# A conditioned block on one core: block 0's inner features in another tile, two groups of operations swapped, one weight load on another queue, weight sums at other places

## The chip, the core and the metric

The kernel runs on one core of one Trainium2 chip. Its time is device microseconds of one execution, taken several times; the median counts. One more execution is recorded by the hardware profiler, and everything said of engines and waits comes from that record. The core has five engines that run side by side, each through its own list of instructions in order: TensorE (PE, the matmuls), VectorE (DVE), ScalarE (ACT), GpSimd (POOL) and SyncE (SP, which here only starts transfers). ACT can start transfers too. [...]

## What is computed

Four sequences' worth of tokens, 2 x 2048 rows of 512 features, go through a block whose scales, shifts and gates come from a condition vector:

```python
emb = jnp.dot(jax.nn.silu(t), ada_w) + ada_b
shift_msa, scale_msa, gate_msa, shift_mlp, scale_mlp, gate_mlp = jnp.split(emb, 6, axis=-1)
norm = _ln(x) * (1.0 + scale_msa[:, None]) + shift_msa[:, None]
h = jax.nn.gelu(jnp.dot(norm, ssm_w1) + ssm_b1, approximate=False)
ssm_out = jnp.dot(h, ssm_w2) + ssm_b2
x = x + gate_msa[:, None] * ssm_out
norm2 = _ln(x) * (1.0 + scale_mlp[:, None]) + shift_mlp[:, None]
hf = jax.nn.gelu(jnp.dot(norm2, ff_w1) + ff_b1, approximate=True)
ff_out = jnp.dot(hf, ff_w2) + ff_b2
x = x + gate_mlp[:, None] * ff_out
```

`ssm_w1` and `ssm_w2` are 512 x 512, `ff_w1` is 512 x 1024, `ff_w2` 1024 x 512, all in float32.

## The kernel before, in words

The 4096 rows are cut into 8 blocks of 512 tokens; blocks 0 to 3 belong to the first sequence, 4 to 7 to the second. A block goes through four products, which the code names by letters: hA (first weight, exact gelu), oA (second weight, added to x), hC (ff's first weight, approximate gelu) and oC (ff's second weight, added to x). Each is done with seven products of half size in place of eight (P1 to P7), for which sums of the operands' quarters are formed beforehand: `sums_of_first` (lines 309 to 312) and `sums_of_second` (319 to 322), four additions each. The seven go in the order P1, P2, P6, P5, P7, P3, P4; in block 0's hA it is P1, P2, P5, P6, P3, P7, P4, and `FIRST` (P1, P2, P5, P6, P7, P3, P4) in block 0's oA and block 1's hA. P1, P6, P7 and P4 accumulate in the PSUM bank "y", P5 and P3 in "v", P2 in "x"; after each one DVE adds the bank's content to its destination (lines 554 to 566 in a hidden product, 598 in a residual one), and the next product of the same bank may start only when that is done.

The order is written out by hand: every engine carries out its instructions in the order in which the code emits them. A dictionary `hooks` holds, for each of P1 to P7, the operations to be emitted right after that product's matmuls; `hook` spreads a list over given places, one each, the last place taking the rest. So the places in the hooks are the places in the lists of DVE, ACT, POOL and SP.

From block 1 on, hC uses a scheme with fewer products over registers (`HK_A`, `HK_B`, `HK_P`): `HK_A` is a program of 37 additions of 128 x 256 elements that turns ff_w1 and its earlier sums, in place, into the combinations that the scheme needs. It runs once, on DVE (`sums_of_registers`, lines 631 and 633), and overwrites fw1_sb and fw1_s; because fw1_sb has already been turned into sums for block 0's hC, ff_w1 is first loaded a second time into the same tile (`load_w` at line 927, 2 MB, on SP). The list `fa_sums` holds the 37; `take(n)` emits the next n: 22 in block 0's oC (line 954), 8 in block 2's hA (line 1007), the rest in block 1's hC. `HK_B` does the like for the tokens, on POOL (also line 633), in the tile `forms`, from block 1 on.

The tiles that matter here:

- `big_tile` gives one of 8 rotating buffers of 1 MB for x, the slices of ada_w, the normalised tokens nT and the inner features hA, hClo, hChi. A new tile waits for the last reader of the buffer's earlier one. Block 0's hA takes one at line 800, right before ada_5.
- `forms` is a tile of its own, not used before block 1.

Around the change stand, in time's order: block 0's hA (to 32 us) with the gate row (`rows_of_gates(2)`: L283 on PE, L292 on DVE, then the matmul `pgate`, L298); block 0's oA with block 1's statistics (`stats`, L419 and L420 on DVE), scales (`scales`, L428 to L446, ten small operations on POOL), normals (`normal`, L459 on ACT), transposes (L488 on PE) and modulation (L502); POOL's sums of w2's and fw1's quarters; block 1's hA from 49 us; then block 0's hC, block 1's oA, block 0's oC (101 to 127 us), block 2's hA. Block 2's normalised tokens nT_2 are turned by DVE (L470) and moved by 16 transfers of 64 KB on SP (`move`, L479); then ACT modulates them (L502). Block 1's second norm, n2_1, goes the same way in block 0's oC, with its 16 moves shared by SP and ACT.

Transfers carry one of eight semaphores in turn, and one that takes a semaphore again waits for the one before on it.

Of the kernel before, what the change touches and what calls it, by code (L numbers as in the profile page):

```python
# [140 lines left out]
def kernel(  # L141
# [16 lines left out]
    nc = tc.nc  # L158
    P = 128
    B, N, D = x.shape  # L160
    H = fw1.shape[1]
    KD = D // P
# [30 lines left out]
    def big_tile(name):  # L193
        return big.tile([P, KD, D], F32, tag="big", name=name)
# [11 lines left out]
    def load_ada(g):  # L206
        ada[g] = big_tile(f"ada_{g}")
        nc.sync.dma_start(
            out=ada[g], in_=ada_w[:, g * D : (g + 1) * D].rearrange("(k p) n -> p k n", p=P)
        )  # L210

    def load_w(name, w, t=None):
        if t is None:
            t = const.tile([P, w.shape[0] // P, w.shape[1]], F32, tag=name, name=name)
        nc.sync.dma_start(out=t, in_=w.rearrange("(k p) n -> p k n", p=P))
        return t

    def load_row(t, row):
# [14 lines left out]
    load_ada(0)  # L233
    load_ada(1)
    w1_sb = load_w("w1", w1)
    load_ada(2)

    nc.gpsimd.memset(brows[:, :2, :], 0.0)
    for n, g in enumerate((2, 5)):
        nc.scalar.dma_start(  # L240
            out=brows[:B, n, :], in_=ada_b[g * D : (g + 1) * D].unsqueeze(0).to_broadcast([B, D])
        )
    w2_sb = load_w("w2", w2)
    b2_bc = work.tile([P, D], F32, tag="gb", name="gb2_0", bufs=2)
    load_row(b2_bc, b2)
    load_x(1)
    load_ada(3)
    load_ada(4)
    fw1_sb = load_w("fw1", fw1)

    mods = {}

    def modulation(g0, part):


        g = g0 + part
        pa = ps_g.tile([P, D], F32, tag="x", name=f"pada_{g}")
        w = ada[g].rearrange("p k (n m q) -> p k m n q", n=KD, q=G)
        for k in range(KD):
            for m in range(P // G):  # L260
                nc.tensor.matmul(
                    pa[m * G : (m + 1) * G, :P],
                    silu[:, k, :],
                    w[:, k, m],
                    start=(k == 0),
                    stop=(k == KD - 1),
                    tile_position=(0, m * G),
                    skip_group_check=True,
                )
        turned = work.tile([P, KD, G], F32, tag="turned", name=f"turned_{g}")  # L270
        nc.vector.transpose(turned.rearrange("p n q -> p (n q)"), pa[:, :P])
        m = const.tile([P, KD, B], F32, tag=f"mod_{g0}_{part}", name=f"mod_{g0}_{part}")
        bias = colsT[:, R_ADA + g * KD : R_ADA + (g + 1) * KD]
        nc.vector.tensor_tensor(m, turned[:, :, :B], bias.unsqueeze(2).to_broadcast([P, KD, B]), ALU.add)
        mods[g0, part] = m
# [124 lines left out]
    def hook(hooks, places, ops):  # L400

        for n, op in enumerate(ops):
            hooks.setdefault(places[min(n, len(places) - 1)], []).append(op)
# [180 lines left out]
    def residual(name, i, hops, wops, kdim, hooks, last=False, order=ORDER):  # L584

        xt = xs[i]
        F = D // 2
        q = {
            "11": xt[:, 0:2, :F],
            "12": xt[:, 0:2, F:],  # L590
            "21": xt[:, 2:4, :F],
            "22": xt[:, 2:4, F:],
        }
        dest = {"P1": "11", "P2": "11", "P6": "12", "P5": "22", "P7": "22", "P3": "12", "P4": "21"}

        def after(p, ps, js):
            d = q[dest[p]][:, js]
            nc.vector.tensor_tensor(d, ps[BANK[p]][:, js], d, ALU.add)  # L598
            if last and p in ("P7", "P4"):
                s = slice(2 + js.start, 2 + js.stop)  # L600
                f = slice(F, D) if p == "P7" else slice(0, F)
                nc.sync.dma_start(out=out_blk[i][:, s, f], in_=xt[:, s, f])

        parted = ("P1", "P6", "P7", "P4") if last else ()
        group(name, kdim, hops, lambda p, j, k: wops[p][:, k, :], after, hooks, parted, order)
# [16 lines left out]

    forms = const.tile([P, 16, C, HT // C], F32, tag="forms", name="forms")

    def sums_of_registers(program, reg, engs):


        def op(n, d, f, a, b):
            eng = engs[n % len(engs)]
            if f == "n":  # L630
                nc.vector.scalar_tensor_tensor(reg[d], reg[a], -1.0, reg[b], ALU.mult, ALU.subtract)
            else:
                eng.tensor_tensor(reg[d], reg[a], reg[b], ALU.add if f == "+" else ALU.subtract)  # L633

        return [lambda z=(n,) + step: op(*z) for n, step in enumerate(program)]
# [93 lines left out]
    def run(ops):  # L729
        for op in ops:  # L730
            op()
# [4 lines left out]
    n1 = {0: Norm(0, 1), 1: Norm(1, 1)}  # L736
# [60 lines left out]
        n1[0].modulate(k, pts[k], nc.vector if k % 2 else None)  # L797
    n1_sums = n1[0].summed(nc.vector)
    run(n1_sums[:2])
    hA_0 = big_tile("hA_0")  # L800
    load_ada(5)
    fw2_sb = load_w("fw2", fw2)
    gb, hA = {2: b2_bc}, {}
# [9 lines left out]
    def fold2(lo, hi):  # L813
        return [lambda k=k: found["w2"][1][k]() for k in range(lo, hi)]

    hooks = {}
    hook(hooks, ("P1",), n1_sums[2:3])
    hook(hooks, ("P2",), [lambda: rows_of_gates(2)] + n1_sums[3:])
    st = n1[1].stats()
    hook(hooks, ("P5",), [ssm_gate, gb2_0] + biases(0, b2_bc) + fold2(0, 1))  # L820
    hook(hooks, ("P6",), fold2(1, 7))
    hook(hooks, ("P3", "P7"), st)
    hook(hooks, ("P7",), [lambda: modulation(3, 0)])
    hA[0] = First(0, n1[0].ops, hooks, ("P1", "P2", "P5", "P6", "P3", "P7", "P4"), hA_0)
    w2_ops = found["w2"][0]

    hA_sums = hA[0].summed(nc.vector)
    hooks = {}
    hook(hooks, ("P1",), [n1[1].scales] + fold2(7, 8) + hA_sums[:2])
    hook(hooks, ("P2",), hA_sums[2:] + [lambda c=c: n1[1].normal(c, on_pe=True) for c in range(C)])  # L830
    hook(hooks, ("P6",), [lambda: modulation(3, 1)])
    hook(hooks, ("P7", "P3", "P4"), n1[1].turned())
# [1 line left out]
    st = n2[0].stats()  # L834
# [7 lines left out]
    hooks = {}  # L842
# [37 lines left out]
    def take(n):  # L880
        ops = fa_sums[:n]
        del fa_sums[:n]
        return ops

    n1[2] = Norm(2, 1)
    for i in range(NBLK):
        nxt, nx2, last = i + 1 < NBLK, i + 2 < NBLK, i + 1 == NBLK
        hC = Second(i)
        if i == 0:
            hooks = first_hooks  # L890
# [3 lines left out]
            hooks = {}  # L894
# [9 lines left out]
        else:  # L904
            hooks = {}
# [16 lines left out]
        hooks = {}  # L922
        hook(hooks, EARLY, hC.summed(1, nc.gpsimd if nxt else nc.vector))
        if nxt:

            if i == 0:
                hook(hooks, ("P1",), [lambda: load_w("fw1", fw1, fw1_sb)])
                fa_sums.extend(sums_of_registers(HK_A, fa, (nc.vector,)))
            if nx2:
                hook(hooks, ("P7",), n1[i + 2].moved())  # L930
            if fold:
                hook(hooks, EARLY, fold[4:8])
                hook(hooks, ("P7",), fold[8:])
            n2[i + 1] = Norm(i + 1, 2)
            hook(hooks, ("P3", "P4"), n2[i + 1].stats())
            residual(f"oA_{i + 1}", i + 1, hA[i + 1], w2_ops, KD // 2, hooks)
        else:
            for p in EARLY:
                run(hooks.get(p, ()))
        fold = None  # L940

        hooks = {}
# [8 lines left out]
            hook(hooks, turns, [lambda c=c: n2[i + 1].turn(c) for c in range(C)])  # L951
            hook(hooks, turns[-1:], [lambda: n2[i + 1].move((nc.sync, nc.scalar))])
        if i == 0:
            hook(hooks, ("P2",) * 2 + ("P6",) * 3 + ("P5",) * 5 + ("P7",) * 6 + ("P3",) * 6, take(22))
        elif i + 3 < NBLK:
            hook(hooks, ("P5", "P7", "P3", "P4"), n1[i + 3].stats())
            hook(hooks, ("P4",), [n1[i + 3].scales])
# [18 lines left out]
        if nxt:  # L976
            late = {}

            def form(eng):

                fb[i + 1] = n2[i + 1].registers()
                return sums_of_registers(HK_B, fb[i + 1], (eng,))

            if not nx2:
                hook(hooks, ("P7",) * 9 + ("P3",) * 6 + ("P4",), [lambda n=n: late_form(n) for n in range(len(HK_B))])

                def late_form(n):
                    if n == 0:
                        late["ops"] = form(nc.vector)
                    late["ops"][n]()  # L990
# [11 lines left out]
        hooks = {}  # L1002
        if refold5:
            hook(hooks, ("P6",), [multiply_5])
        if i == 0:
            hook(hooks, ("P5", "P7", "P3", "P4"), n1[i + 3].stats())
            hook(hooks, ("P1", "P2", "P2", "P6", "P6", "P5", "P7", "P3"), take(8))
        if refold2:
            w2_ops, w2_fold = weight_of_second(w2_sb, w2_s, gate[2, b], (nc.vector,))
            hook(hooks, ALL, w2_fold)  # L1010
# [47 lines left out]
```

## Time and profile before

| | |
|---|---|
| median of 3 runs | 608.75 us (608.74 to 609.2) |
| the profiled execution | 609.73 us, its span 607.9 us |
| PE busy | 98% of the span |
| DVE, ACT, POOL busy | 61%, 35%, 65% |
| DMA queue q1 (SP) | 45.63 MB, 22.1% of 16 engines |
| DMA queue q10 (ACT) | 3.70 MB, 2.4% |

A line of the timeline reads: start in us from the span's start, duration in us, engine, line of the kernel, operation, output tile <- input tiles, shapes, number of instructions, and in brackets the time that the engine stood idle before it with what ended that idle time. A line of the waits reads: engine, output tile and line, what it waited for, then us in total, how often, longest. Buffer numbers are left out of names, so hA is that of any block and fw is any of the tiles of ff_w1 and ff_w2. A wait on several semaphores is put down to the one that came last by the record.

### The profile page before, as it was taken

Reading aid. Unit: us, or ns where it says so; the run is one execution under the profiler, and the core shown is the slowest. Engines: PE = TensorE matmul, PEld = TensorE weight load, DVE = VectorE, ACT = ScalarE, POOL = GpSimd, SP = SyncE. Lnnn points to the kernel's source line nnn. Section 1 sums busy time; section 2 is a strip of 40 time slices with the busy share of each in tenths; the row PEclk is TensorE's granted clock in tenths of the full one; section 3 lists DMA queues with packets and bytes.
Section 4 is the critical chain, followed back from the end, with each engine's and each line's share of the span. In section 5 each row is a group of like instructions: output and inputs, shape, how many; then the busy total and the mean of one; then the engine's idle time right before and its main releaser. Section 6 shows DMA issues by size and latency. Waiting matters only on the chain.

```text
span 607.9 us, 8128 instructions
## 1 busy us (share of the span) xinstructions
PE 593.7 (98%) x2843; PEld 511.4 (84%) x2843; DVE 371.1 (61%) x638; ACT 214.7 (35%) x355; POOL 394.7 (65%) x446
## 2 busy tenths in 40 slices
PE   7999999989999999999999999999999999999997
PEld 3678888778888888888888888888888888888886
DVE  4887785799754456555755458744575236467642
ACT  2233341134711455322642337213553225212420
POOL 2796589878736598438997398895993695540110
PEclk9999999999999999999999999999999999999999
DMA  8971005410132102430042520321020300012001
GB/s 323 414 269 70 1 2 183 159 73 1 27 112 71 69 2 64 162 104 36 1 98 81 159 98 18 122 65 74 1 52 18 104 36 0 1 44 96 1 1 70
DMA packets 22605, 49.85 MB, mean 82 GB/s; under 512 B 4084, under 2 KB 4640, under 8 KB 21668
## 3 DMA queue, kind: packets, MB, share of 16 engines
q1 hardware_dynamic: 19792, 45.63, 22.1%
q10 hardware_dynamic: 2772, 3.70, 2.4%
q8 instruction: 23, 0.38, 0.3%
q14 instruction: 18, 0.15, 0.1%
HBM read 27.29 MB, written 8.39 MB: 59 GB/s over the span
## 4 chain that ended last, share of the span: by engine, by line
PE 79%; DVE 10%; POOL 5%; DMA 2%; issue 2%; ACTq 1%; ACT 0%; SPq 0%; DVEq 0%; POOLq 0%
PE py_oC L385 14%; PE px_hC L694 9%; PE pv_hC L694 8%; PE py_hA L385 8%; PE py_oA L385 8%; PE py_hC L694 7%; PE pv_oC L385 7%; PE pv_oA L385 4%; PE px_oC L385 3%; PE pv_hA L385 3%; PE px_hA L385 2%; DMA ada<-in_L_cond_ada_w_dram 2%; PE px_oA L385 2%; DVE fw L633 1%; DVE fw_s L633 1%
## 5 line engine op out<-in xcount | busy, mean ns | idle before, releaser
L610 POOL TENSOR_TENSOR x<-x,gb 128x512 f32<-128x512 f32 x64 | 80.0, 1280 | 7.6 <-ACT hA L557 3.8
L502 ACT ACTIVATE nT<-nT,mod,mod 128x512 f32<-128x512 f32 x50 | 36.7, 803 | 122.0 <-DMA nT<-blocks 112.0
L459 ACT ACTIVATE nT<-x,nmr,rstd 128x512 f32<-128x512 f32 x52 | 39.6, 804 | 58.1 <-POOL nmr L446 42.2
L428 POOL TENSOR_SCALAR ve<-mv 128x4 f32<-128x4 f32 x16 | 3.7, 233 | 86.2 <-DVE mv L420 86.0
L385 PE MATMUL py_oC<-fw_s,hSC 128*128 128x256 f32 x256 | 57.9, 379 | 0.0
L385 PEld LDWEIGHTS py_oC<-fw_s,hSC 128*128 128x128 f32 x256 | 48.6, 190 | 6.6
L309 POOL TENSOR_TENSOR hSC<-hClo 128x512 f32<-128x512 f32 x15 | 19.1, 1275 | 47.7 <-ACT hClo L689 38.6
L419 DVE BATCH_NORM_STATS2 st<-x 128x6 f32<-128x512 f32 x64 | 43.4, 678 | 5.7 <-DMA x<-in_x_dram 5.4
L598 DVE TENSOR_TENSOR x<-py_oC,x 128x512 f32<-128x512 f32 (+1 forms) x36 | 22.6, 630 | 37.5 <-PE py_oC L385 37.1
L694 PE MATMUL py_hC<-forms,fw 128*128 128x256 f32 x168 | 40.8, 379 | 0.0
L705 DVE TENSOR_TENSOR hClo<-hClo,py_hC 128x512 f32<-128x512 f32 x42 | 28.7, 682 | 17.5 <-ACT hClo L708 9.1
L470 DVE STREAM_TRANSPOSE blocks<-nT 128x512 f32<-128x512 f32 x52 | 35.2, 695 | 5.1 <-ACT nT L459 4.7
L633 POOL TENSOR_TENSOR forms<-forms 128x256 f32<-128x256 f32 x48 | 35.4, 737 | 2.8
L694 PEld LDWEIGHTS py_hC<-forms,fw 128*128 128x128 f32 x168 | 31.9, 190 | 4.3
L598 DVE TENSOR_TENSOR x<-py_oA,x 128x512 f32<-128x512 f32 x32 | 22.1, 690 | 21.2 <-PE py_oA L385 19.3
L705 DVE TENSOR_TENSOR hChi<-hChi,pv_hC 128x512 f32<-128x512 f32 x35 | 23.4, 684 | 16.9 <-PE pv_hC L694 16.9
L385 PE MATMUL py_hA<-nS,w_s 128*128 128x256 f32 x128 | 30.4, 380 | 1.7 <-POOL forms L633 1.7
L385 PE MATMUL pv_oC<-fw,hSC 128*128 128x256 f32 x128 | 29.0, 380 | 1.4 <-DVE x L598 1.4
L385 PE MATMUL py_oA<-w_s,hSA 128*128 128x256 f32 x128 | 30.3, 380 | 0.0
L385 PEld LDWEIGHTS py_hA<-nS,w_s 128*128 128x128 f32 x128 | 24.2, 190 | 6.6 <-POOL forms L633 2.1
L689 ACT ACTIVATE hClo<-hClo,colsT 128x256 f32<-128x256 f32 x56 | 25.4, 500 | 11.8 <-DVE hClo L705 11.7
L385 PE MATMUL px_oC<-fw,hChi 128*128 128x256 f32 x128 | 28.9, 379 | 0.0
(206 smaller groups left out, 1431.3 us busy)
## 6 DMA issues: line engine op xcount, KB each, us to landing
nT<-blocks SPq DMA_DIRECT2D x152, 64.0 KB, 2.0
fw<-in_L_cond_ff_w_dram SPq DMA_DIRECT2D x4, 2048.0 KB, 9.0
out_dram<-x SPq DMA_DIRECT2D x15, 512.0 KB, 3.1
x<-in_x_dram SPq DMA_DIRECT2D x7, 1024.0 KB, 7.1
ada<-in_L_cond_ada_w_dram SPq DMA_DIRECT2D x6, 1024.0 KB, 10.5
nT<-blocks ACTq DMA_DIRECT2D x56, 64.0 KB, 2.1
w<-in_L_cond_ssm_w_dram SPq DMA_DIRECT2D x3, 1024.0 KB, 7.8
x<-in_x_dram SPq DMA_DIRECT2D x2, 512.0 KB, 5.9
```

Source lines behind the costliest of these rows:

```text
L309: lambda: eng.tensor_tensor(s[1], q["11"], q["21"], ALU.subtract),
L385: nc.tensor.matmul(ps[b][j * apart][:, j, :], lhs(p, j, k), rhs(p, j, k), start=(fresh and j * (not apart) == 0 and k == 0), stop=(p in (" ...
L419: nc.vector.bn_stats(st, xs[self.i][:, c, :])
L459: nc.scalar.activation(t, x_c, AF.Identity, bias=self.nmr[:, c : c + 1], scale=self.rstd[:, c : c + 1])
L470: nc.vector.transpose(self.bl[:, :, :, c, :].rearrange("p m k q -> p k m q"), self.nT[:, c, :].rearrange("p (k m q) -> p k m q", k=KD, m=C),)
L502: nc.scalar.activation(dst, src, AF.Identity, bias=shift, scale=scale)
L598: nc.vector.tensor_tensor(d, ps[BANK[p]][:, js], d, ALU.add)
L610: lambda c=c: nc.gpsimd.tensor_tensor(xs[i][:, c, :], xs[i][:, c, :], gb, ALU.add)
L633: eng.tensor_tensor(reg[d], reg[a], reg[b], ALU.add if f == "+" else ALU.subtract)
L689: nc.scalar.activation(h, h, AF.Gelu_apprx_tanh, bias=fb1T[:, m : m + 1])
L694: nc.tensor.matmul(ps[b][:, j, :], fa[ra][:, j * P : (j + 1) * P], fb[rb].rearrange("p a (c q) -> p c a q", q=Q), start=(fresh and j == 0) ...
L705: nc.vector.tensor_tensor(dest(d), dest(d), ps[b], op)
```

## The change

There are five edits. Block 0's hA no longer takes a big tile but the first half of `forms`. In the hooks of block 0's hA only two of block 1's four statistics stay; the other two go to the head of P1's hooks of oA, ahead of the scales; and the first two sums of hA_0, which stood behind the scales and one weight sum in those hooks, are emitted right after hA. The second load of ff_w1 is started by ACT instead of SP. The first 22 of the `HK_A` sums in block 0's oC go to P1 (6), P5 (7), P7 (7) and P3 (2), where they were at P2 (2), P6 (3), P5 (5), P7 (6) and P3 (6). In block 2's hA seven are taken instead of eight (one at P6 less).

```diff
-    def load_w(name, w, t=None):
+    def load_w(name, w, t=None, eng=nc.sync):
...
-        nc.sync.dma_start(out=t, in_=w.rearrange("(k p) n -> p k n", p=P))
+        eng.dma_start(out=t, in_=w.rearrange("(k p) n -> p k n", p=P))
...
     forms = const.tile([P, 16, C, HT // C], F32, tag="forms", name="forms")
+
+    hA_0 = forms[:, :8].rearrange("p n a r -> p (n a r)").rearrange("p (k t) -> p k t", k=KD)
...
     run(n1_sums[:2])
-    hA_0 = big_tile("hA_0")
     load_ada(5)
...
-    hook(hooks, ("P3", "P7"), st)
+    hook(hooks, ("P3", "P7"), st[:2])
...
     hA_sums = hA[0].summed(nc.vector)
+    run(hA_sums[:2])
     hooks = {}
-    hook(hooks, ("P1",), [n1[1].scales] + fold2(7, 8) + hA_sums[:2])
+    hook(hooks, ("P1",), st[2:] + [n1[1].scales] + fold2(7, 8))
...
-                hook(hooks, ("P1",), [lambda: load_w("fw1", fw1, fw1_sb)])
+                hook(hooks, ("P1",), [lambda: load_w("fw1", fw1, fw1_sb, nc.scalar)])
...
-            hook(hooks, ("P2",) * 2 + ("P6",) * 3 + ("P5",) * 5 + ("P7",) * 6 + ("P3",) * 6, take(22))
+            hook(hooks, ("P1",) * 6 + ("P5",) * 7 + ("P7",) * 7 + ("P3",) * 2, take(22))
...
-            hook(hooks, ("P1", "P2", "P2", "P6", "P6", "P5", "P7", "P3"), take(8))
+            hook(hooks, ("P1", "P2", "P2", "P6", "P5", "P7", "P3"), take(7))
```

On the engines this moves the following. DVE: in block 0 the order becomes two statistics, the turn and sum of mod_3_0 (L271, L274), hA_0's two sums (L309, L310), L598 of P1, two statistics, L598 of P2, L311, L312. ACT: the load stands between the last activation of block 0's hC (L570) and the modulation of nT_2 (L502). SP: its list loses the load, and the eighth of nT_2's 16 moves takes the semaphore that the load carries, so it waits for the load to land. PE and POOL keep their order.

## The prediction

> **What bounds the kernel now.** I read the page first: busy shares, then the waits of PE, longest first, and last the timeline of 12 to 64 us and 95 to 150 us, where every one of those waits lies. PE is busy for 593.7 of 607.9 us, so nothing but its 14 us of idle time can be won, and only the part that this change touches. All times below are us from the span's start.
>
> ```profile
> PE 593.7 (98%) x2843; PEld 511.4 (84%) x2843; DVE 371.1 (61%) x638; ACT 214.7 (35%) x355; POOL 394.7 (65%) x446
> ...
> PE py_hA L385 <- POOL forms L633: 1.7, 1, 1.7
> ...
> PE pv_oC L385 <- DVE x L598: 1.4, 1, 1.4
> ...
> PE pgate L298 <- DVE grows L292: 1.2, 1, 1.2
> PE pv_oA L385 <- POOL rstd L444: 1.0, 1, 1.0
> ```
>
> These four waits (5.3 us) are the change's whole field. The timeline names the true causes:
>
> ```profile
> 20.10 0.69 DVE L554 TENSOR_TENSOR hA<-py_hA,colsT 128x512 f32<-128x512 f32 x1 [1.20 <-PE pada L283]
> 23.19 1.13 PE L298 MATMUL pgate<-grows,pick_bc 128*128 128x512 f32 x2 [1.23 <-DVE grows L292]
> ...
> 36.26 0.69 DVE L310 TENSOR_TENSOR hA<-hA 128x512 f32<-128x512 f32 x1 [0.53 <-DVE hSA L309]
> 37.09 1.97 PE L385 MATMUL pv_oA<-w,hA 128*128 128x256 f32 x8 [1.04 <-POOL rstd L444]
> 37.37 0.25 POOL L446 TENSOR_SCALAR nmr<-nmr 128x4 f32<-128x4 f32 x1
> ...
> 42.14 2.35 POOL L310 TENSOR_TENSOR fw<-fw 128x1024 f32<-128x1024 f32 x1
> 42.22 2.30 DVE L274 TENSOR_TENSOR mod<-turned,colsT 128x8 f32<-128x8 f32 x1
> ...
> 47.02 2.37 POOL L312 TENSOR_TENSOR fw_s<-fw,fw_s 128x1024 f32<-128x1024 f32 x1
> ...
> 50.01 0.69 DVE L319 TENSOR_TENSOR nS<-nT 128x512 f32<-128x512 f32 x1 [1.08 <-ACT nT L502]
> ...
> 108.10 0.69 DVE L598 TENSOR_TENSOR x<-px_oC,x 128x512 f32<-128x512 f32 x1 [2.69 <-PE px_oC L385]
> ...
> 119.81 3.72 PE L385 MATMUL pv_oC<-fw,hSC 128*128 128x256 f32 x16 [1.39 <-DVE x L598]
> ...
> 131.36 0.67 DVE L554 TENSOR_TENSOR hA<-py_hA,colsT 128x512 f32<-128x512 f32 x1
> 132.18 1.97 PE L385 MATMUL py_hA<-nS,w_s 128*128 128x256 f32 x8 [1.74 <-POOL forms L633]
> ```
>
> To be seen: hA_0 lies in ada_2's buffer, so DVE may not write it until PE's L283 has read ada_2 (1.20 idle), and the gate row L292 and pgate come late. pv_oA starts 0.14 after DVE's L310 ends (36.95), so L310 is what it waits for; POOL's rstd is a chance neighbour. At 132.18 it is DVE's L554 that frees PSUM bank y, late because L633 sums stand ahead of it. And L274, a tiny operation, takes 2.30 beside a big POOL one, and ends with it.
>
> **What the Trainium skill says.** "SBUF — State Buffer", section "SBUF: two separate sides": GpSimd and a DVE operation with two SBUF inputs take one port pair as an exclusive lock for the whole instruction; the other blocks. The trace agrees: L274 ends 0.03 after POOL's L310; 512-element operations end 0.55 after the POOL operation (L320 18.90 against 18.35, L312 39.83 against 39.29), the 256-element sums L633 about 0.26 after, one per POOL operation (116.27, 1.49 long). L598 reads PSUM and is never blocked (0.68 throughout). "DMA: Bandwidth & Descriptors", section "Issuing engines are not separate DMA queues": transfers issued by ACT and SP run on the same 16 engines and interleave. No stretch of before has a large load on ACT's queue.
>
> **Part 1, hA_0 into forms.** L554 waits for py_hA alone. DVE: L554 18.93 to 19.6; L321 behind POOL's L311 (ends 20.03) to 20.58; L556, L292 to 21.85. pgate can start at 21.96, when PE is free: the 1.23 goes, and all up to oA_0's P2 is 1.24 earlier. No load is late for that: x_1 landed by 22.0, ada_3 by 24.5. Every later big tile takes the buffer one place earlier in the rotation; the waits that follow are for ada loads long landed, and x_2's load (48.08) goes out about 7 earlier, needed at 69. Worth 0.
>
> **Part 2, statistics and sums swapped** (times with the 1.24 taken off). DVE's statistics of c=1 end at 30.13. L271 to 30.35; L274 behind POOL's L320 to 31.53; L309 to 32.2 (or 33.4 if POOL takes the lock first); L310 to 33.9 to 34.1. pv_oA may start at 34.8: no wait. But then L598, two statistics (0.86 each), L598 and only then L311, ending at 37.4 to 37.6, where P6 wants it at 36.4: a new stall of 1.0 to 1.2 for the 1.04 removed. Worse, mv of block 1 is complete at 36.1 to 36.4, where before it stood at 32.95 and POOL was the later (34.18). POOL's scales (3.07 uncontended, L428 at 106.12 to L446 at 109.19; 0.3 more for collisions) end at 39.3 to 39.85, against 37.62. ACT's four normals (2.93) end about 42.7; the first transposes want the last at 42.4: 0.3. Behind the scales on POOL stand L322 of w2 (1.28) and four sums of fw1 (9.7: four of 2.4 and gaps), so these end at N + 11.0 = 50.3 to 50.85, before 49.39. There lies the price: block 1's L319 is ready at 48.9 and before found POOL idle; now the last fw1 sum has the lock, L319 ends 0.55 after it, 50.85 to 51.4, before 50.70. From L319 to L559 (56.74) DVE ran without a gap, and PE's P7 at 56.80 waited for L559. So P7 moves by +0.15 to +0.7: I take +0.45. All of part 1's gain is gone, and block 0 to 105 runs 0.45 late: n2_0's scales, normals and transposes follow the same chain.
>
> **Part 3, fw1 on ACT's queue** (before's times again; the 0.45 shifts all). ACT is free at 89.94, and has nothing to do until L502 at 101.77. SP's issue of the same load took 0.52; first packets came 1.2 after it, all had landed 8.0 after it. With seven moves of 64 KB between them (0.45 MB at about 0.35 MB/us, half of it counted): landing at 98.6. SP no longer issues it, so x_3's load is issued after the moves alone. But the built order has a new wait: the semaphore of the eighth nT_2 move is fw1's, so SP holds moves 8 to 16 until fw1 has landed: 98.6 instead of 94.43. Behind it on SP stand nine moves and x_3's load; for the moves ACT's L502 waits. L502 moves from 101.77 to 105.9, ends 108.9. Its cover: n2_1's normals could not start before 109.23. Cost 0, with 0.6 in hand; beyond that each us goes into the normals.
>
> **Part 4, sums spread.** Six L633 sums go into the 2.69 idle before 108.10: the first behind POOL's hSC (106.04) to 106.3, five of 0.44 to 108.5. POOL's scales lose 0.35, normals start at 109.55, turns end at 113.65 (115.5 before, no sums between them), moves and forms follow 1.9 earlier (forms 123.6). L598 of P5 at 115.0: the 1.39 at P3 goes. The next seven sums meet POOL's four L610: four end one per L610 (to 120.75), three of 0.42 to 121.95; L598 of P7 ends 122.6, P4 wanted 121.7: new stall 0.9; P4 stands at 122.6, before 123.37. Seven more: four free, three at 0.85 beside forms, to 126.45; L598, two sums, L598, L554 to 129.75. P6 of hA_2 then starts at 129.8 to 131 (before 132.18): the unlucky end is when forms start before the sums are through. P7 and P4 keep it: P4 at 137.3 to 138.5, before 139.59: gain 1.1 to 2.3, I take 2.0. hA_2 has seven sums for eight; the one that moves into hC_1 stands beside POOL's hSA: 0.2 back. Net -1.8.
>
> **Sum.** +0.45 - 1.8 = -1.35 on the profiled execution's 609.73 (span 607.93 and 1.80 around it): 608.4. The median of the runs is 0.98 below that execution: 607.4.
>
> **Rivals.** (a) No change to be measured: the sums get no free lock. The seven after P5 and seven after P7 are both slowed by POOL (0.85 to 1.37 each), part 4 brings 1.1 - 0.2, part 2 costs 0.45 to 0.7: 608.3. For: the lock decides twice within 0.3 us. Against: forms come earlier only if the turns do, and then POOL's L610 is as early. (b) Slower: the fw1 load on ACT's ring shares 16 engines with the moves, and SP's moves wait for it. Place: SP's eighth move. If it lands at 101.5 rather than 98.6, normals and turns start 1.8 late and part 4 keeps 0.4; from there each us is paid in full by turns, sums and L598 of P6, which stand in one line on DVE. Landing at 103.5 (5 us lost): +0.45 + 2.0 - 0.4 = +2.05, 610.8. For: such sharing was never run in before. Against: fw1 is 6.4 us of packets and the seven moves 1.2. (c) POOL done earlier: if the collisions fall kindly and fw1's sums end by 48.9, L319 is not blocked, part 1 stays won (-1.2), and with part 4 it gives 605.8. Against: it needs at least 1.4 us out of a chain of 11.
>
> **Numbers.** 0.2% (1.22 us) is about what a measurement of this kernel can tell from no change. Forecast 0.42 (own range 606.4 to 608.0; 0.39 of it counts as faster, 0.03 as same), (a) 0.32, (b) 0.20, (c) 0.06. Faster 0.45, same 0.35, slower 0.20. The range runs from (c) to short of (b)'s full price: 605.6 to 609.9.
>
> **What would show it.** Right: no wait of pgate or pv_oA; a wait of py_oA on DVE's L311 near 37; POOL's last fw1 sum past 50 and DVE's L319 long (over 2 us) beside it; py_hA at about 57.3; SP's moves in two bursts with a hole of 4 us; no wait of pv_oC, one of py_oC's P4 below 1.2. Wrong: L319 short (then c), L502 for nT_2 later than 106.6 after the shift (then b), or P6 of hA_2 not earlier than 131.5 (then a). A wait in blocks 2 to 7, whose code is unchanged, would upset the whole sum.

## The result and the profile after

| | median | lowest to highest | runs |
|---|---|---|---|
| before | 609.0 us | 607.41 to 609.34 | 8 |
| changed | 607.16 us | 606.9 to 607.58 | 8 |

The ratio is 0.9974, its 95% interval 0.9963 to 0.9984. A second, larger set (20 executions of the changed kernel, 33 of the one before) gave 607.07 against 608.67 and a ratio of 0.9981 [0.9973, 0.999]. The change makes the kernel faster by 0.2 to 0.3%. The profiled execution took 607.58 us, with a span of 605.8.

The page's busy line and then the waits of PE, both of the changed kernel. A wait gives us in total, how often, and the longest. Lines of the code below the new hA_0 have moved down by two (the sums are L633 and L635 now, two lines of one helper, and hC's product is L696).

```profile
PE 593.8 (98%) x2843; PEld 511.2 (84%) x2843; DVE 370.9 (61%) x638; ACT 214.8 (35%) x355; POOL 394.7 (65%) x446
```

```profile
PE py_oA L385 <- DVE hSA L311: 0.8, 1, 0.8
PE px_hC L696 <- DVE hChi L707: 0.7, 2, 0.5
...
PE pv_hA L385 <- DVE nT L320: 0.6, 1, 0.6
PE py_oC L385 <- DVE x L598: 0.6, 1, 0.6
PE py_hA L385 <- DVE hA L559: 0.6, 1, 0.6
PE px_hC L696 <- DVE hClo L707: 0.5, 1, 0.5
```

PE's work is the same 593.8 us. The four waits shown of before (pgate 1.2, pv_oA 1.0, pv_oC 1.4, py_hA 1.7) are gone. Five smaller ones, 3.1 us in all, stand in their place: for L311, L320, L598, L559 and hClo. The two of px_hC for hChi were there before as well, with 0.6. The timeline of the changed kernel shows the places, in the order of the steps:

```profile
20.92 1.12 PE L298 MATMUL pgate<-grows,pick_bc 128*128 128x512 f32 x2
...
35.06 0.23 POOL L428 TENSOR_SCALAR ve<-mv 128x4 f32<-128x4 f32 x1 [2.85 <-DVE mv L420]
...
36.29 1.97 PE L385 MATMUL py_oA<-w_s,hSA 128*128 128x256 f32 x8 [0.78 <-DVE hSA L311]
...
46.99 2.36 POOL L312 TENSOR_TENSOR fw_s<-fw,fw_s 128x1024 f32<-128x1024 f32 x1
47.66 2.24 DVE L319 TENSOR_TENSOR nS<-nT 128x512 f32<-128x512 f32 x1 [1.08 <-ACT nT L502]
...
50.68 1.99 PE L385 MATMUL pv_hA<-nT,w 128*128 128x256 f32 x8 [0.64 <-DVE nT L320]
...
55.99 1.99 PE L385 MATMUL py_hA<-nS,w_s 128*128 128x256 f32 x8 [0.59 <-DVE hA L559]
...
88.30 0.41 ACTq L215 DMA_DIRECT2D fw<-in_L_cond_ff_w_dram  x1
...
97.88 5.57 SPq L479 DMA_DIRECT2D nT<-blocks  x9
...
104.51 0.97 DVE L635 TENSOR_TENSOR fw<-fw 128x256 f32<-128x256 f32 x1
105.10 2.94 ACT L502 ACTIVATE nT<-nT,mod,mod 128x512 f32<-128x512 f32 x4 [15.97 <-DMA nT<-blocks]
...
108.54 2.94 ACT L459 ACTIVATE nT<-x,nmr,rstd 128x512 f32<-128x512 f32 x4 [0.51 <-POOL nmr L446]
...
121.66 3.72 PE L385 MATMUL py_oC<-fw_s,hChi 128*128 128x256 f32 x16 [0.60 <-DVE x L598]
...
128.71 1.97 PE L385 MATMUL py_hA<-nS,w_s 128*128 128x256 f32 x8
```

To be seen: pgate starts without a wait (an idle time would stand in brackets). POOL sat idle 2.85 until block 1's mv was complete, so its last fw1 sum runs to 49.35, and DVE's L319, ready at 47.66, is held for 2.24 in place of 0.69 and ends 0.55 after POOL's. DVE's next operations are late with it: P5 of hA_1 (50.68) waits 0.64 for L320, and P7 (55.99) 0.59 for L559. In the second half, SP has issued seven of nT_2's 16 moves by 93.59 and the other nine from 97.88 on, when ACT's load has landed (97.87). In before the same nine followed the first seven at once:

```profile
94.43 5.65 SPq L479 DMA_DIRECT2D nT<-blocks  x9
```

ACT finishes L502 for nT_2 and waits 0.51 more for POOL before the normals: the late moves were covered, with half a microsecond to spare. P6 of hA_2 (128.71) has no stall.

**A ledger.** PE is busy 98% of the span, so a shift of its products tells where time is won. For each of PE's groups of products (some 340) I took its start in a kernel's timeline minus that in the timeline of before, and noted where the difference steps. The start of the run is left out: the profiled execution of before reached its first transposes 0.92 us later than that of the changed kernel, through its first loads, and some executions start later still (last section). That is no effect of the change.

```
us, change of PE's shift     changed  part 1  parts 1+2  parts 3+4
pgate                         -1.36   -1.40    -1.38       0
P5 of oA_0 (pv_oA)            -1.20   -0.43    -1.20       0
P6 of oA_0, then to 44        +1.13    0       +1.12       0
P5 to P7 of hA_1 (50 to 57)   +1.54    0       +1.54       0
P3 of oC_0                    -1.56    0        0         -1.56
P4 of oC_0, P1 of hA_2        +0.76    0        0         +0.76
P6 of hA_2                    -1.87    0       -0.42      -1.98
P4 of hA_2                    -0.51    0       -0.50      -0.50
hC_1 (150 to 155)             +1.21    0       +0.32      +1.33
block 7, px_hC                +0.32   +0.25    +0.09      -0.28
```

The rows of the changed kernel come to -1.54, with the start to about -2.5; the spans differ by 2.15, since the stretch after PE's last product was 0.35 us longer than in before. The steps of one edit repeat from kernel to kernel within 0.15 us. The last row does not: two profiled executions of the changed kernel agree within 0.1 us from the first transposes up to there and then part by 0.75, at a wait of px_hC for ACT's hClo of which one shows 0.7. No edit touches that place. Medians and ledger of one execution can therefore differ by about 1 us, and I use the ledger for where, and medians of one set of runs for how much.

### The profile page after: what moved, and what is told of

Same layout as the page of the kernel before. It is cut to its first block, busy times and chain, and to the rows that moved or that the text cites. A ratio compares the mean times of both kernels' runs of the same rounds, so it can differ in the third digit from the quotient of the medians.

```text
span 605.8 us, 8128 instructions
## 1 busy us (share of the span) xinstructions
PE 593.8 (98%) x2843; PEld 511.2 (84%) x2843; DVE 370.9 (61%) x638; ACT 214.8 (35%) x355; POOL 394.7 (65%) x446
## 4 chain that ended last, share of the span: by engine, by line
PE 86%; DVE 8%; DMA 2%; issue 1%; ACTq 1%; ACT 1%; POOL 0%; SPq 0%; DVEq 0%
PE py_oC L385 15%; PE px_hC L696 9%; PE py_oA L385 9%; PE py_hA L385 8%; PE pv_hC L696 8%; PE pv_oC L385 7%; PE py_hC L696 7%; PE pv_oA L385 4%; PE pv_hA L385 4%; PE px_oC L385 4%; PE py_hC L385 2%; PE px_oA L385 2%; PE px_hA L385 2%; DMA ada<-in_L_cond_ada_w_dram 2%; PE pv_hC L385 1%
## 5 line engine op out<-in xcount | busy, mean ns | idle before, releaser
L502 ACT ACTIVATE nT<-nT,mod,mod 128x512 f32<-128x512 f32 x50 | 36.7, 802 | 123.1 <-DMA nT<-blocks 114.7
L309 POOL TENSOR_TENSOR hSC<-hClo 128x512 f32<-128x512 f32 x15 | 19.1, 1277 | 48.7 <-ACT hClo L691 38.9
L598 DVE TENSOR_TENSOR x<-py_oC,x 128x512 f32<-128x512 f32 (+1 forms) x36 | 22.6, 630 | 37.6 <-PE py_oC L385 37.2
L696 PE MATMUL py_hC<-forms,fw 128*128 128x256 f32 x168 | 41.1, 380 | 0.0
L635 POOL TENSOR_TENSOR forms<-forms 128x256 f32<-128x256 f32 x48 | 35.8, 747 | 2.8
L696 PEld LDWEIGHTS py_hC<-forms,fw 128*128 128x128 f32 x168 | 31.8, 190 | 4.7 <-DVE hClo L707 0.4
L598 DVE TENSOR_TENSOR x<-py_oA,x 128x512 f32<-128x512 f32 x32 | 22.1, 690 | 21.2 <-PE py_oA L385 19.6
L385 PE MATMUL py_oC<-fw_s,hChi 128*128 128x256 f32 x128 | 29.0, 380 | 0.6 <-DVE x L598 0.6
```

The lines of the kernel that those rows point to most:

```text
L309: lambda: eng.tensor_tensor(s[1], q["11"], q["21"], ALU.subtract),
L385: nc.tensor.matmul(ps[b][j * apart][:, j, :], lhs(p, j, k), rhs(p, j, k), start=(fresh and j * (not apart) == 0 and k == 0), stop=(p in (" ...
L502: nc.scalar.activation(dst, src, AF.Identity, bias=shift, scale=scale)
L696: nc.tensor.matmul(ps[b][:, j, :], fa[ra][:, j * P : (j + 1) * P], fb[rb].rearrange("p a (c q) -> p c a q", q=Q), start=(fresh and j == 0) ...
```

## The experiments

Two theories stood behind the first four. A is the chain of the prediction: late statistics, late scales on POOL, the port lock at L319, a small net for the start; and the gain in the spread sums. B put it elsewhere, as each expectation says. The first four ran beside one set of the kernel before (608.28 us median, 42 executions).

**1. Part 1 alone.**

```diff
+    hA_0 = forms[:, :8].rearrange("p n a r -> p (n a r)").rearrange("p (k t) -> p k t", k=KD)
...
-    hA_0 = big_tile("hA_0")
```

> Part 1 alone (hA_0 in forms). Theory A (the lock chain): pgate no longer waits, and since block 1's statistics, POOL's scales and fw1's sums keep their places, POOL is idle when block 1's L319 starts; the 1.2 to 1.36 us stay won to the end: 1.2 us faster than before, hA_1's P7 some 1.3 earlier. Theory B (the gain of block 0 is absorbed somewhere before 105 us whatever part 2 does): 0 us.

Measured: 607.37 us, ratio 0.9986 [0.9978, 0.9993]. pgate moves by 1.40, pv_oA by another 0.43, and nothing is given back: no further step of the ledger reaches 0.1 us before block 7, so the new rotation of the big tiles cost nothing that PE saw. The timeline of this kernel, where the statistics keep their place:

```profile
31.80 0.23 POOL L428 TENSOR_SCALAR ve<-mv 128x4 f32<-128x4 f32 x1
...
44.77 2.36 POOL L312 TENSOR_TENSOR fw_s<-fw,fw_s 128x1024 f32<-128x1024 f32 x1
47.22 0.69 DVE L319 TENSOR_TENSOR nS<-nT 128x512 f32<-128x512 f32 x1 [1.08 <-ACT nT L502]
```

POOL gets mv at 31.80 and not at 35.06, its last sum is over at 47.13, and L319 at 47.22 takes 0.69. It escapes by 0.09 us.

**2. Parts 1 and 2.** To the edit of experiment 1 comes

```diff
-    hook(hooks, ("P3", "P7"), st)
+    hook(hooks, ("P3", "P7"), st[:2])
...
+    run(hA_sums[:2])
...
-    hook(hooks, ("P1",), [n1[1].scales] + fold2(7, 8) + hA_sums[:2])
+    hook(hooks, ("P1",), st[2:] + [n1[1].scales] + fold2(7, 8))
```

> Parts 1 and 2 (tile and swap), load and sums as before. Theory A: both waits (pgate, pv_oA) are gone and both come back, at P6 of oA_0, P5 and P7 of hA_1, because POOL's fw1 sums end late and hold the port against L319: 0 us (from -0.3 to +0.4) against before, 1.2 slower than part 1 alone. Theory B (the swap is worth its 1.0 us): 2.2 us faster than before.

Measured: 609.05 us, ratio 1.0019 [1.001, 1.0028]. Part 2 thus costs 609.05 - 607.37 = 1.68 us. The ledger has the same swing by 57 us: from -1.83 with part 1 to +0.08; by the end of the run the two are 1.2 us apart. Its timeline shows the lock as in the changed kernel:

```profile
46.98 2.36 POOL L312 TENSOR_TENSOR fw_s<-fw,fw_s 128x1024 f32<-128x1024 f32 x1
47.64 2.24 DVE L319 TENSOR_TENSOR nS<-nT 128x512 f32<-128x512 f32 x1 [1.07 <-ACT nT L502]
```

Compared with before, the two parts together are a loss of 0.77 by the medians, outside theory A's range, where the ledger's rows come to -0.43. That difference stays open.

**3. Parts 3 and 4.**

```diff
-                hook(hooks, ("P1",), [lambda: load_w("fw1", fw1, fw1_sb)])
+                hook(hooks, ("P1",), [lambda: load_w("fw1", fw1, fw1_sb, nc.scalar)])
...
-            hook(hooks, ("P2",) * 2 + ("P6",) * 3 + ("P5",) * 5 + ("P7",) * 6 + ("P3",) * 6, take(22))
+            hook(hooks, ("P1",) * 6 + ("P5",) * 7 + ("P7",) * 7 + ("P3",) * 2, take(22))
...
-            hook(hooks, ("P1", "P2", "P2", "P6", "P6", "P5", "P7", "P3"), take(8))
+            hook(hooks, ("P1", "P2", "P2", "P6", "P5", "P7", "P3"), take(7))
```

> Parts 3 and 4 (fw1's second load on ACT, sums spread, 7 for 8), tile and order of block 0 as before. Theory A: all that the change wins lies here: 3.2 us won up to hA_2's P4, 1.2 given back in block 1's hC, 2.0 us faster than before. Theory B (the profile's gain is mostly in the start of the run and in block 0): under 0.5 us.

Measured: 606.49 us, ratio 0.9972 [0.9961, 0.9983], 1.79 us below before. By the ratios, practically the whole gain of the change is in these two parts.

**4. The changed kernel without part 2.**

```diff
-    hook(hooks, ("P3", "P7"), st[:2])
+    hook(hooks, ("P3", "P7"), st)
...
-    run(hA_sums[:2])
...
-    hook(hooks, ("P1",), st[2:] + [n1[1].scales] + fold2(7, 8))
+    hook(hooks, ("P1",), [n1[1].scales] + fold2(7, 8) + hA_sums[:2])
```

> The changed kernel with part 2 undone (parts 1, 3, 4). Theory A: -1.2 and -2.0 add up: 3.2 us faster than before, 1.3 faster than the changed kernel; L319 of block 1 takes 0.7, not 2.2. Theory B (the swap is worth 1.0): 0.8 to 1.0 slower than the changed kernel.

Measured: 605.63 us, ratio 0.9963 [0.9949, 0.9976]. It is 0.86 below parts 3 and 4 alone, as part 1 was 0.91 below before, and 1.5 below the changed kernel, which ran in another set; L319 again takes 0.69.

**5. Is it the chain on POOL, or only late normals?** In the changed kernel POOL idles 2.85 us while a ready sum of w2 (L322) stands behind the scales. Here it goes ahead of them:

```diff
-    hook(hooks, ("P1",), st[2:] + [n1[1].scales] + fold2(7, 8))
+    hook(hooks, ("P1",), st[2:] + fold2(7, 8) + [n1[1].scales])
```

> The changed kernel, with POOL's sum of w2 (L322, 1.3 us) put ahead of block 1's scales, into the 2.85 us for which POOL waits for mv. Theory A (part 2 loses by a chain on POOL: late scales, then L322, then four sums of fw1 that hold the port lock when L319 is ready): the last fw1 sum ends about 1.3 us earlier (48.0 for 49.35), L319 ends 0.6 to 1.3 us earlier (49.9 at 47.66 + 2.24 in the changed kernel), the stall of P7 of hA_1 (0.59 for hA L559) shrinks by as much, and the kernel takes 0.5 to 1.3 us less than the changed one: 606.0 to 606.7. Theory B (the late statistics hold back the normals on ACT and the transposes, and POOL's sums are not what decides): L319 starts no earlier, and the time stays within 0.3 us of the changed kernel's.

Measured: 606.18 us, ratio 0.9965 [0.9951, 0.998], about 1 us below the changed kernel, which ran in another set. The timeline (this execution started about 1.5 us late):

```profile
33.77 1.60 POOL L322 TENSOR_TENSOR w_s<-w,w_s 128x512 f32<-128x512 f32 x1
36.54 0.23 POOL L428 TENSOR_SCALAR ve<-mv 128x4 f32<-128x4 f32 x1 [1.17 <-DVE mv L420]
...
47.23 2.36 POOL L312 TENSOR_TENSOR fw_s<-fw,fw_s 128x1024 f32<-128x1024 f32 x1
...
49.13 1.00 DVE L319 TENSOR_TENSOR nS<-nT 128x512 f32<-128x512 f32 x1 [1.07 <-ACT nT L502]
```

L322 fills POOL's idle time, and L319 is held for 0.3 us and not for 1.55. Against the changed kernel, PE's shift steps by -0.81, -0.11 and -0.33 at P5 to P7 of hA_1: 1.25 of the 1.54 us come back. The statistics are as late as in the changed kernel, so theory B falls.

**6. Part 3 taken back**, in the changed kernel:

```diff
-                hook(hooks, ("P1",), [lambda: load_w("fw1", fw1, fw1_sb, nc.scalar)])
+                hook(hooks, ("P1",), [lambda: load_w("fw1", fw1, fw1_sb)])
```

> All of the change except part 3: fw1's second load is issued by SP again. Theory A (the place of the load is hidden either way, and what counts is when fw1 has landed against the six sums of P1): within 0.6 us of the changed kernel, 606.6 to 607.8; SP's moves of nT_2 go out without the hole of about 4 us, ACT's L502 for nT_2 starts about 4 us earlier (101 to 102 in place of 105.1), and the normals of nT_2 (L459, 108.54) stay where they are. Theory B (part 3 carries part of the gain): 1 us or more slower than the changed kernel, with the P1 sums of fw1 waiting for the load. Theory C (part 3 costs something through the hole): 0.5 us or more faster than the changed kernel, with the normals of nT_2 earlier than 108.54.

Measured: 608.42 us, ratio 0.9992 [0.9981, 1.0003]. The moves go out without the hole and the normals keep their place (110.64, in an execution that runs 2.1 us late: 108.5), as A said. But the time is 1.3 us above that of the changed kernel, and the first spread sum waits 2.8 us for the load, as B said; A's time does not hold. Since the two ran in different sets, I repeated both in one.

> The changed kernel once more, beside the version with the load on SP. Both theories: 606.9 to 607.6, ratio to before 0.996 to 0.9985.

Measured for the changed kernel: 607.07 us, ratio 0.9981 [0.9973, 0.999].

> The version without part 3 once more, on the same chip as the changed kernel. Theory A (part 3 is worth what the ledger of its trace shows: the six sums of P1 wait for the load, which lands about 3 us later, and then meet POOL): 0.2 to 0.7 us slower than the changed kernel. Theory B (the two medians of the calls so far, 608.42 and 607.16, are right, part 3 is worth 1.1 us or more): 1.0 to 1.5 us slower than the changed kernel.

Measured without part 3: 608.07 us, ratio 0.9995 [0.9984, 1.0006]. Beside part 4's sums, part 3 is worth 1.00 us, at B's lower edge. The timeline of this execution, which runs 1.3 us late:

```profile
100.66 0.52 SPq L215 DMA_DIRECT2D fw<-in_L_cond_ff_w_dram  x1
...
108.97 0.42 DVE L635 TENSOR_TENSOR fw<-fw 128x256 f32<-128x256 f32 x1 [3.10 <-DMA fw<-in_L_cond_ff_w_dram]
...
109.99 1.52 DVE L635 TENSOR_TENSOR fw_s<-fw 128x256 f32<-128x256 f32 x1
111.55 1.38 DVE L635 TENSOR_TENSOR fw_s<-fw_s,fw 128x256 f32<-128x256 f32 x1
112.85 1.49 DVE L635 TENSOR_TENSOR fw_s<-fw 128x256 f32<-128x256 f32 x1
...
116.78 3.32 PEld L385 LDWEIGHTS py_oC<-fw_s,hSC 128*128 128x128 f32 x16 [1.75 <-DVE x L598]
```

SP issues the load behind all 16 moves, at 100.66 (ACT issues it at 88.30). It lands some 8 us later, the six sums start at 108.97 instead of 104.51, three of them run beside POOL's operations at 1.4 to 1.5 us each, and P7 of oC_0 waits for L598. Against the changed kernel, PE's shift steps in this execution by +1.51 there and by -0.97 from P4 to hA_2's P5; in the first one, where four of the six sums were through before POOL came and not three, by +0.14 there and by +0.10 and +0.19 at P3 and P4. In both, px_hC in hC_1 then waits 1.0 for hClo and not 0.5. By the end of hC_1 the loss is 1.4 us in this execution and 0.6 in the first; the median lies between.

**7. The sum that moved into hC_1.** In the changed kernel hA_2 takes eight sums again, so that none is left over:

```diff
-            hook(hooks, ("P1", "P2", "P2", "P6", "P5", "P7", "P3"), take(7))
+            hook(hooks, ("P1", "P2", "P2", "P6", "P6", "P5", "P7", "P3"), take(8))
```

> The changed kernel, with the eighth sum of fw1 done in hA_2 (a second one at P6) and not in hC_1. Theory A (the 1.2 us that hC_1 gives back hang on the one sum of 1.48 us that stands beside POOL's hSA and ahead of hClo): the stall of px_hC for hClo L707 (0.5) goes, hC_1's product starts 0.6 to 0.7 us less late, nothing is lost in hA_2 (DVE is idle for 0.7 us there), and the time is 0.5 to 1.0 us below the changed kernel's: 606.2 to 606.7. Theory B (hC_1 is late because hA_2 is early and meets POOL's work there anyway): the stall stays at 0.5 or moves to another product of hC_1, and the time is within 0.3 us of the changed kernel's.

Measured: 606.27 us, ratio 0.9963 [0.9949, 0.9977], 0.8 to 0.9 below the two medians of the changed kernel. First the changed kernel's timeline, then this one's:

```profile
146.99 1.33 POOL L312 TENSOR_TENSOR hSA<-hA,hSA 128x512 f32<-128x512 f32 x1
147.12 1.48 DVE L635 TENSOR_TENSOR fw<-fw 128x256 f32<-128x256 f32 x1
...
148.53 0.67 DVE L707 TENSOR_TENSOR hClo<-hClo,px_hC 128x512 f32<-128x512 f32 x1
...
149.26 1.13 PE L696 MATMUL px_hC<-forms,fw_s 128*128 128x256 f32 x4 [0.51 <-DVE hClo L707]
```

```profile
147.36 1.34 POOL L312 TENSOR_TENSOR hSA<-hA,hSA 128x512 f32<-128x512 f32 x1
147.48 0.67 DVE L707 TENSOR_TENSOR hClo<-hClo,px_hC 128x512 f32<-128x512 f32 x1
...
148.94 1.03 PE L696 MATMUL px_hC<-forms,fw_s 128*128 128x256 f32 x4
```

One sum, held to 1.48 us by POOL's L312, stood ahead of the DVE operation that frees px_hC's bank. Without it hClo starts 1.05 us earlier, although POOL's L312 is 0.37 later. The ledger gets back 0.68, 0.10 and 0.29: 1.07 of the 1.21 us. Ahead of that the eighth sum costs 0.16 in hA_2, and hC_1 begins 0.18 later.

**8. Both losses out.** Without part 2 (as in 4) and with the eighth sum in hA_2 (as in 7):

> The changed kernel without part 2 (statistics and sums of block 0 in the order of before) and with the eighth sum in hA_2. Theory A (both losses are independent and add): about 0.6 us below the version without part 2 alone, which took 605.63: 604.7 to 605.4, and faster than both the kernel before and the changed one. Theory B (hC_1's loss is not the sum's): as the version without part 2, 605.3 to 606.0.

Measured: 605.54 us, ratio 0.9945 [0.9927, 0.9964]. Its median lies in B's range, but three of its six executions had started late. It was run once more, in the set of the repeated changed kernel.

> The version without part 2 and with the eighth sum in hA_2 once more, on the same chip as the changed kernel. Theory A (two independent losses taken out): 604.3 to 605.5, 2.0 us or more below the changed kernel. Theory B (the single median of 605.54 was a lucky one): less than 1.5 us below the changed kernel.

Measured: 604.39 us (603.96 to 606.67, 6 executions), ratio 0.9938 [0.9922, 0.9953]; the changed kernel in the same set took 607.07, the one before 608.67. A holds: this version beats both kernels, by 2.7 and 4.3 us. Singly the two edits brought 1.5 and 0.8 to 0.9, so neither takes the other's gain. Its ledger by part: -1.77 at the start, -3.08 from oC_0 to hA_2, +0.32 in hC_1.

## Why the prediction came out right, and which terms were off

The forecast was 607.4, the result 607.16, faster by an amount that the interval separates from nothing. The sum of -1.35 compares with -1.6 to -1.84 by the medians and -1.86 in the ledger without block 7. By the set of the first four experiments, and 6:

| term | put at | measured |
|---|---|---|
| part 1, alone | -1.24 | -0.91 (ledger -1.83) |
| part 2 | +1.69 (from -1.24 to +0.45) | +1.68 (ledger +1.91 by 57 us, +1.15 in all) |
| part 3, beside part 4 | 0 | -1.0 |
| part 4 | -1.8 | -0.8, not run alone (-1.79 for both, less part 3) |

Part 1: pgate's wait went, at 1.36 for 1.24. One small gain was missed: alone, the part also takes 0.43 from pv_oA's wait, which falls from 1.04 to 0.61. Why the medians show only half of the ledger's 1.83 is open. It is not special to part 1: in that set parts 1+2 and parts 3+4 too lie above their whole ledgers (+0.77 for -0.43, -1.79 for -2.23), and the kernel before was faster there (608.28) than in the other sets (608.67 to 609.0). That points to the one execution of before from which every ledger starts, and does not show it. A reading was off without effect: the prediction has x_1 and ada_3 landed by 22.0 and 24.5, where the trace of before has 23.85 and 26.31, still ahead of their first use.

Part 2: each link came as worked out. py_oA waits for L311 (0.78 where 1.0 to 1.2 was put), POOL's last sum ends late, L319 is held, and P7 of hA_1 is late. In the clock of before, that is with the 0.92 of the start added, POOL ends at 50.27 (put at 50.3 to 50.85) and P7 starts at 56.91 (56.95 to 57.5): just below the low end of each. PE paid for it at P5 as well as at P7, which the prediction alone had named. So parts 1 and 2 give +0.11 in the ledger instead of +0.45. "SBUF — State Buffer", section "SBUF: two separate sides", in the Trainium skill, on which this step rested, is borne out: 2.24 for 0.69 beside POOL's 2.36, and 0.69 in the versions where POOL is done by then (experiments 1 and 4).

Part 3: the hole in SP's moves came, and L502 for nT_2 went to 105.10, which is 105.91 in the clock of before (the shift there is 0.81) and was put at 105.9. The cover in hand was 0.51, put at 0.6. The interleaving that the Trainium skill describes in "DMA: Bandwidth & Descriptors", section "Issuing engines are not separate DMA queues", agrees with the trace: the first and the seventh move landed 5.8 and 5.6 us after their issue beside the load, where 2.0 was usual, and the load 9.6 after its own, where it took 8.0 in before. It landed at 98.7 in the clock of before (put at 98.6), PE saw nothing of it, and so rival (b) did not happen. What was wrong is the word "0" for the part: part 4's six sums at 104 to 108 need the load, and the prediction used its new landing without crediting part 3 for it. With the load on SP the sum waits 3.10 for it, and more than half of the gain of parts 3 and 4 is gone (1.0 of 1.79). The total was right, its division was not.

Part 4: two terms were mis-sized and nearly cancel. The gain, put at 1.1 to 2.3 and taken as 2.0, is 3.18 in the ledger (-1.56 + 0.76 - 1.87 - 0.51). P4's stall is 0.60 for 0.9, and P6 of hA_2 starts at 129.52 in the clock of before, with no stall, where the lucky end was 129.8: as forecast, seven of the fourteen sums after P5 and P7 ran free at 0.42, and the rest of DVE's chain was tighter than put. P4 of hA_2 gained 0.5 beyond P6; experiment 2 shows the same 0.5 without part 4. The traces show why. In before the sum behind L559 starts 0.05 us after a POOL operation (134.79 and 134.74) and takes 0.95; in experiment 2 and in the changed kernel it starts 0.06 and 0.12 ahead of one (133.55 and 133.61, 131.32 and 131.44) and takes 0.41. L563 is earlier by as much, and P4's wait of 0.27 for it is gone. The give-back in hC_1, put at 0.2, is 1.21; experiment 7 shows that one sum is 1.07 of it. The step that failed: that sum was priced by its own length, without asking what stands behind it on DVE. POOL's lock makes it 1.48 us, and behind it stands the operation that frees PE's bank. That the two errors, each of 1.0 to 1.2, cancel is luck.

Of the other rivals, (a) needed the fourteen sums to be slowed throughout, and half were not. (c) needed POOL done by 47.66, when L319 was ready; it ended at 49.35, and experiments 1 and 4 show what the difference is worth.

## What to carry to other kernels

When small operations are moved into idle time of one engine, price each by what waits behind it there, and by whether the partner on the shared port is busy at that time: the same sum was 0.42 us in one slot and 1.48 in another. Ask of every part of a change which other part's price assumes it, and never write 0 for a transfer whose earlier landing is used elsewhere in the sum. And when a swap fills one engine's gap but delays a second engine's input, look for ready work that the second engine can do while it waits: one sum put ahead of the scales gave back most of what the swap had cost.

## What the runs showed that was not expected

The start of the same program varies. Windows of the first 15 us in two executions of the version of experiment 8 show how; the columns after the length are busy time by engine, the granted clock, the DMA share and GB/s. The first:

```profile
0.00:15.00 15.00, 11.10 (x83) 6.24 (x84) 6.29 (x23) 3.60 (x6) 3.79 (x12) 0.89 0.89 325
```

and the second:

```profile
0.00:15.00 15.00, 12.10 (x94) 6.84 (x95) 7.50 (x25) 4.73 (x7) 3.69 (x12) 1.00 0.89 325
```

The loads moved as much, but the granted clock of PE was 0.89 in the first and 1.00 in the second. In the first, the first transposes' sixteen products took 2.65 us and not 1.97, the first product of hA_0 started at 15.96 and not at 14.51, and the run stayed some 1.9 us behind. The same holds for all five profiled executions that started late in this way (experiments 4, 5, 6 with its repeat, and the first run of 8): their record has the full clock from 4.4 to 5.1 us on, then half of it for 3.4 us from 11.2 to 11.9 on. In the other eight the full clock is on record from 5.6 to 7.1 us on, and it holds. What decides between the two is not known from these runs.

It matters for reading them. The mean granted clock of the whole execution tells the late ones among the thirteen profiled: it is 0.997 in the five and 0.999 or 1.000 in the eight, and the executions without a profile have the same two groups (0.996 or 0.997, and 0.999 or 1.000). (A start that is late through the loads alone, as that of the profiled execution of before, does not show in it.) These are the medians without the lower group, each against before in the same set:

```
us                                kernel    before   difference
part 1                            607.17    608.19     -1.02
parts 1+2                         608.80    608.19     +0.61
parts 3+4                         606.49    608.19     -1.70
without part 2 (4)                605.32    608.19     -2.87
w2's sum first (5)                605.84    608.71     -2.87
without part 3 (6)                608.00    608.71     -0.71
without part 3, repeated          607.89    608.58     -0.69
eighth sum in hA_2 (7)            606.27    608.71     -2.44
both losses out (8)               604.47    608.71     -4.24
both losses out, repeated         604.30    608.58     -4.28
changed kernel, repeated          606.89    608.58     -1.69
```

The two runs of the last version, 605.54 and 604.39 above, now agree, and no reading of the experiments changes its sign. Parts 1 and 2 alone stand out: by themselves they cost 0.61, yet the change as a whole is no slower than parts 3 and 4. The ledger gives +0.11 for them within the change. Why they cost more alone is open.
